# Pacing of the side work of an attention slot: complete at 0.8 of the slot in place of 0.74

## The chip, the cores and the metric

One core of one Trainium2 chip. The metric is device time in microseconds (us), the median of repeated executions. The engines are TensorE (PE in the profile: matmuls and transposes; PEld are its weight loads), VectorE (DVE), ScalarE (ACT), GpSimd (POOL) and SyncE (SP), which only issues transfers here.

## The reference

Input x is 8 images of 512 channels, 32x32 positions, f32. Two layers run one after the other, each on a group-normalised copy of its input and added to it:

```
x = x + cv2(concat(y0, y1, y2, y3))         # layer 0, input group_norm(x)
    y0, y1 = halves of silu(bn(conv1x1(gn(x))))          # "cv1", 512 -> 512
    z      = silu(bn(conv3x3(y)))                        # "cv1" of block i, 256 -> 256
    z      = attention(z): q, k, v = conv1x1(z); 4 heads of 64, 1024 positions
             softmax(q . (k + r) / 8) times v
    y_next = y + silu(bn(conv1x1(z)))                    # "m_cv2"; blocks i = 0, 1
    cv2    = silu(bn(conv1x1(...)))                      # 1024 -> 512
x = x + conv1x1(group_norm(x)), with masked, scaled and permuted weights   # layer 1
```

## The kernel before

**Slots, units, steps.** The two blocks of eight images are 16 *slots* (L737 to L741). The images go in pairs, in the order (first image, block 0), (second, 0), (first, 1), (second, 1). The attention of a slot is cut into four *units* (pair of heads, half of the query positions), and each unit into eight key tiles t, which are taken two at a time. The loop over slots runs over the four units j of a slot (from L1048 on). A unit does `top` (L524: the running maxima are transposed into a PSUM bank, L530, and reduced, L531), `spread` (L533: the negated maxima are transposed back into `mb`, L539), and then for each pair of key tiles `soften` (L544, DVE adds `mb` to the logits), `exponent` (L548, ACT; L555, POOL sums), `values` (L562, `po`, of the pair before) and the *next* unit's `logits` (L510, with the ACT copy L517 out of PSUM and the DVE maximum L522). `finish` and `divide` (L571 to L585) close the unit before. So the logits of the next slot begin in the last unit of this one, at its first pair of key tiles: they need that slot's q and k.

**Side work.** All that is not attention is fed between these steps by generators, which yield after every few matmuls and give their estimated time in us. `slot_filler` (L912 to L947) lists them for slot s: background work of other images (`bg.take`: first 1x1 convolutions, `cv2`, layer 1), the 1x1 convolution behind the attention (`conv_m2`), the 3x3 convolution of the next slot (`conv3`, L294: six products of 12 matmuls each, L313, over *planes* that DVE and POOL make from the input, L280 to L285 and L340 to L346), the next slot's q, k and v (`project`, L377, L405), and at the end as much background work as fills the slot up to `SHARE`, 103. The sum without that last entry is `needed`, the sum with it `total`. From the entries' estimates, `needed` is 8 + 7 + 9 + 32 + 7 + 21 = 84 in the slots whose next slot is a block 1 (s = 1, 2, 5, 6, 9, 10, 13, 14), 75 in the others, 68 in slot 0 and 15 in slot 15, which has no next slot.

**The pace.** `advance(share)` (L1041) pulls from that list until the done estimate reaches a goal, the larger of two: `share` of `total`, and a faster share of `needed`. A slot has 4 x 10 steps; with base = 10 j, `advance` is called at (base + 0.7)/40 ahead of `top`, (base + 1.4)/40 ahead of `spread`, (base + 2)/40 behind it, and (base + 4 + t)/40 behind each pair of key tiles. In the last unit (base 30) these are 30.7, 31.4, 32 (0.8 of the slot, right ahead of the pair in which the next slot's first logits are issued), 34, 36, 38 and 40 of 40.

**What sets the order on the engines.** The order in the program is the order on each engine. `pe_turn` (L196), `act_turn` (L188) and `in_turn` (L182) keep the attention's instructions, and the transforms of DVE, in the order in which they are written. A clock of estimated us (L743) starts further work when it is due: DVE's plane transforms by a list with a gap between its entries (`Spread`, L204), group norm's steps, and loads. `Background.take` (L867) overshoots by a part of a group and takes what it overshot from its next share (`over`, L870).

**PSUM.** Logits, transposed maxima, denominators and all side work share five banks (L63, `bank`, L68), which are used in turn; a group of matmuls can start only when ACT or DVE has emptied the bank five before it. `mb` and `po` have their own.

**ACT's functions.** `copy` and `mul` can run at any time; SiLU (L130) and the exponential (L548) use two tables, and a program that goes from one to the other contains a table load (ACT_TABLE_LOAD).

Of the kernel before, what the change touches and what calls it, by code (L numbers as in the profile page):

```python
# [39 lines left out]
def conv_preact_kernel(ctx: ExitStack, tc: tile.TileContext, x, cv1, cv2, mcv1, qkv, mcv2, bn, rw, rh, conv, s_in, t_in, out):  # L40
# [871 lines left out]
    def slot_filler(s):  # L912

        prev = slots[s - 1] if s else (None, 0)
        nxt = slots[s + 1] if s + 1 < len(slots) else (None, 0)
        todo, needed = [], 0.0

        def add(us, g):
            nonlocal needed
            todo.append((us, g))  # L920
            needed += us

        im, i = nxt
        add(8.0, bg.take(8.0))
        if im and i == 1:
            add(7.0, im.conv_m2(0))
            add(0.0, call(im.transform, 1, 2.0, 3.3))
            add(9.0, bg.take(9.0))
        products = im.conv3(i) if im else iter(())
        if prev[1] == 1:  # L930
            if im:
                add(21.3, (us for _, us in zip(range(16), products)))
            add(7.0, prev[0].conv_m2(1))
            add(0.0, call(lambda: finishing(prev[0])))
        if im:
            add(10.7 if prev[1] == 1 else 32.0, products)
            add(7.0, bg.take(7.0))
        if im:
            add(21.0, im.project(i))
        if s + 2 < len(slots) and slots[s + 2][1] == 0:  # L940
            add(0.0, call(slots[s + 2][0].load_y))
            add(0.0, call(slots[s + 2][0].transform, 0, 8.0, 3.3))
        rest = SHARE - needed if im else 70.0
        if rest > 0:
            todo.append((rest, bg.take(rest, wait=True)))
        total = sum(c for c, _ in todo)
        return needed, total, todo  # L947
# [77 lines left out]
    for s in range(len(slots)):  # L1025
        needed, total, todo = slot_filler(s)
        state = {"done": 0.0}

        def filler():
            for us, g in todo:  # L1030
                start = state["done"]
                for cost in g:
                    clock.tick(cost)
                    state["done"] += cost
                    yield

                state["done"] = max(state["done"], start + us)

        fill = filler()

        def advance(share):  # L1041
            goal = max(share * total, min(1.0, share / 0.74) * needed + 0.1)
            while state["done"] < goal:
                if next(fill, "end") == "end":
                    break

        steps = 4 * (KT + 2)
        for j in range(4):  # L1048
            u = units[4 * s + j]
            nxt = units[4 * s + j + 1] if 4 * s + j + 1 < len(units) else None  # L1050
            base = j * (KT + 2)

            advance((base + 0.7) / steps)
            u.top()
            clock.tick(0.9)
            advance((base + 1.4) / steps)
            u.spread()
            clock.tick(0.9)
            advance((base + 2) / steps)
            for t in range(0, KT, 2):  # L1060
                if before and t == 0:
                    before.finish()
                    clock.tick(0.9)
                u.soften(t)
                u.soften(t + 1)
                if t:
                    u.exponent(t)

                lag = u if t else before
                if lag:  # L1070
                    lag.values((t - 2) % KT)
                    lag.values((t - 1) % KT)
                    clock.tick(2.0)
                if before and t == 0:
                    before.divide(0)
                    before.divide(1)
                if nxt:
                    nxt.logits(t)
                    nxt.logits(t + 1)
                    clock.tick(2.0)  # L1080

                if not t:
                    u.exponent(t)
                u.exponent(t + 1)
                advance((base + 4 + t) / steps)
            before = u
        for _ in fill:
            pass
# [62 lines left out]
```

## Time and profile before

| what | value |
|---|---|
| median of 3 runs | 3153.09 us (3151.32 to 3154.78) |
| the profiled execution's own time | 3162.82 us |
| its span, first to last instruction | 3161.1 us |
| mean granted TensorE clock | 0.996 |
| PE busy | 3077.0 us (97%) |
| DVE busy | 2049.9 us (65%) |
| ACT busy | 1721.0 us (54%) |
| POOL busy | 1398.4 us (44%) |
| ACT table loads | 224, of 1283 ns each |

A row such as "L548 ACT ... x512 | 539.1, 1068 | 304.1" is a group of instructions of one line: how many, busy us together, mean ns of one, and the idle us of that engine ahead of them with what ended it. In a timeline row the first two numbers are the start and the duration of a run of like instructions, and brackets hold idle time ahead of it with the instruction that ended it.

### The profile page before, as it was taken

The numbers are of one execution on the slowest core, as the hardware profiler recorded it, in microseconds if no ns is written. First come the engines' busy times: TensorE is split into PE (matmuls) and PEld (weight loads), VectorE is DVE, ScalarE is ACT, GpSimd is POOL, SyncE is SP. The second block draws the span as 40 slices with busy tenths as digits, with TensorE's granted clock in tenths as the row PEclk, the third lists the DMA queues.
The fourth block names the chain that finished last, engine by engine and source line by source line (L and its number), as shares of the span: only waits on it lengthen the run. The fifth ranks groups of instructions, "written<-read, shape, count | busy, mean of one in ns | idle before, by whom it ended". The sixth has DMA issues, their size and how long they took to land.

```text
span 3161.1 us, 34185 instructions
## 1 busy us (share of the span) xinstructions
PE 3077.0 (97%) x11668; PEld 1515.3 (48%) x11668; DVE 2049.9 (65%) x2718; ACT 1721.0 (54%) x2349; POOL 1398.4 (44%) x1867
## 2 busy tenths in 40 slices
PE   7999999998999999999999999999999999999999
PEld 3645354454445454455445454454445454453333
DVE  5446577567667576667666676767666676767642
ACT  3245765855655555644656455544656455546621
POOL 2104444546444554455444454445444464444520
PEclk9999999999999999999999999999999999999999
DMA  8852352421233232424233332424233332413356
GB/s 289 292 182 74 130 180 87 153 77 63 88 116 131 79 128 71 149 84 148 84 116 130 114 127 70 153 85 136 91 110 130 120 120 70 150 64 120 120 205 217
DMA packets 142014, 399.35 MB, mean 126 GB/s; under 512 B 13072, under 2 KB 14352, under 8 KB 141840
## 3 DMA queue, kind: packets, MB, share of 16 engines
q1 hardware_dynamic: 141120, 396.94, 36.6%
q8 instruction: 92, 1.51, 0.2%
q14 instruction: 82, 0.67, 0.1%
q10 hardware_dynamic: 720, 0.23, 0.0%
HBM read 317.42 MB, written 79.69 MB: 126 GB/s over the span
## 4 chain that ended last, share of the span: by engine, by line
PE 75%; DVE 4%; ACT 4%; issue 2%; DMA 1%; POOL 1%; SPq 0%; ACTq 0%; DVEq 0%; POOLq 0%
PE cv L175 15%; PE m L313 13%; PE po L562 12%; PE lg L510 12%; PE l L175 7%; PE qk L175 6%; PE v L405 3%; PE m L175 3%; PE den L576 2%; PE mb L539 2%; PE mt L530 1%; ACT st L517 1%; DVE st L544 1%; ACT st L548 1%; DVE mx L522 1%
## 5 line engine op out<-in xcount | busy, mean ns | idle before, releaser
L555 POOL TENSOR_TENSOR sum<-sum,st 128x256 f32<-128x256 f32 x1536 | 1132.0, 771 | 552.1 <-ACT st L548 547.7
L522 DVE TENSOR_TENSOR mx<-mx,lg 128x512 f32<-128x512 f32 x768 | 477.8, 682 | 417.6 <-ACT st L517 417.4
L517 ACT COPY st<-lg 128x512 f32<-128x512 f32 x1024 | 525.0, 597 | 356.1 <-PE lg L510 331.7
L548 ACT ACTIVATE st<-st 128x1024 f32<-128x1024 f32 x512 | 539.1, 1068 | 304.1 <-DVE st L544 302.9
L544 DVE TENSOR_TENSOR st<-st,mb 128x1024 f32<-128x1024 f32 x512 | 604.4, 1215 | 60.2 <-PE mb L539 60.2
L555 POOL TENSOR_TENSOR sum<-st,st 128x256 f32<-128x256 f32 x256 | 185.1, 754 | 788.8 <-ACT st L548 788.8
L313 PE MATMUL m<-plane,w_m 128*128 128x256 f32 x2304 | 528.8, 383 | 4.9 <-ACT cv2s L130 2.7
L562 PE MATMUL po<-st,v 128*64 128x512 f32 x2048 | 497.8, 605 | 18.2 <-ACT st L548 16.2
L510 PE MATMUL lg<-q,k 64*128 64x512 f32 x2048 | 510.9, 617 | 2.9 <-ACT y L130 2.9
L313 PEld LDWEIGHTS m<-plane,w_m 128*128 128x128 f32 x2304 | 426.4, 189 | 129.5 <-issue 45.1
L175 PE MATMUL cv<-y,w_cv 128*128 128x512 f32 x1024 | 464.5, 599 | 7.9 <-ACT cv2s L130 4.6
L510 PEld LDWEIGHTS lg<-q,k 64*128 64x128 f32 x2048 | 177.3, 186 | 328.2 <-issue 267.4
L175 PEld LDWEIGHTS cv<-y,w_cv 128*128 128x128 f32 x1024 | 185.8, 190 | 248.1 <-issue 226.4
L562 PEld LDWEIGHTS po<-st,v 128*64 128x64 f32 x2048 | 128.8, 136 | 323.6 <-issue 237.3
L175 PE MATMUL cv<-x,w_cv 128*128 128x512 f32 x512 | 237.0, 610 | 10.6 <-ACT y L130 3.7
L175 PE MATMUL l<-x,w_l 128*128 128x512 f32 x512 | 236.9, 606 | 7.9 <-DVE mx L522 6.9
L175 PE MATMUL qk<-z,w_qkv 128*128 128x512 f32 x512 | 234.0, 600 | 1.4 <-DVE mx L522 1.4
L583 DVE RECIPROCAL rb<-rb 128x256 f32<-128x256 f32 x128 | 215.5, 1723 | 26.0 <-ACT rb L579 25.8
L531 DVE TENSOR_REDUCE nm<-mt 128x4 f32<-128x512 f32 x128 | 82.3, 684 | 144.7 <-PE mt L530 144.7
L579 ACT COPY rb<-den 128x512 f32<-128x512 f32 x64 | 37.3, 583 | 230.4 <-PE den L576 230.4
L175 PEld LDWEIGHTS cv<-x,w_cv 128*128 128x128 f32 x512 | 95.3, 194 | 132.0 <-issue 109.3
L175 PEld LDWEIGHTS l<-x,w_l 128*128 128x128 f32 x512 | 93.4, 191 | 130.4 <-issue 112.2
(145 smaller groups left out, 2408.8 us busy)
## 6 DMA issues: line engine op xcount, KB each, us to landing
w_m<-w_m SPq DMA_DIRECT2D x96, 768.0 KB, 4.8
w_cv<-in_cv SPq DMA_DIRECT2D x90, 512.0 KB, 3.5
y<-y SPq DMA_DIRECT2D x64, 512.0 KB, 4.8
x<-in_x SPq DMA_DIRECT2D x56, 512.0 KB, 5.2
y<-y SPq DMA_DIRECT2D x64, 256.0 KB, 3.5
k<-r SPq DMA_DIRECT2D x32, 512.0 KB, 3.6
res<-y SPq DMA_DIRECT2D x32, 512.0 KB, 4.0
xr<-in_x SPq DMA_DIRECT2D x32, 512.0 KB, 4.1
```

The costliest lines, as they stand in the source:

```text
L175: nc.tensor.matmul(ps, w, moving, start=(n == 0), stop=(n == len(terms) - 1))
L313: nc.tensor.matmul(ps[:, ts(co, 256)].rearrange("p (t x) -> p t x", x=F), w[:, co, c, dx], u[:, 9 * c : 9 * c + 8, dx : dx + F], start=(j ...
L405: nc.tensor.matmul(ps[:, ts(j, P)], z[:, c, ts(4 * j4 + j, P)], w[:, c, 512 + P * hp : 512 + P * hp + P], start=(c == 0), stop=(c == IT - 1),)
L510: nc.tensor.matmul(lg[h], self.k[r, ts(t, P)], self.q[r, self.hp, ts(self.half, HALF)], start=True, stop=True)
L517: act_turn(nc.scalar.copy(st[:, h], lg[h]))
L522: in_turn(nc.vector.tensor_tensor(self.mx[:, h], so_far[:, h], lg[h], ALU.max))
L531: nc.vector.tensor_reduce(self.nm[:, h], mt, AX.X, ALU.max, negate=True)
L544: in_turn(nc.vector.tensor_tensor(st, st, flat(self.mb), ALU.add))
L548: act_turn(nc.scalar.activation(st, st, AF.Exp))
L555: nc.gpsimd.tensor_tensor(flat(self.acc)[:, part], flat(so_far)[:, part], st[:, part], ALU.add)
L562: nc.tensor.matmul(self.po[HD * h : HD * h + HD], self.v[:, t, ts(h, HD)], self.st[t][:, h], start=(t == 0), stop=(t == KT - 1),)
L583: nc.vector.reciprocal(self.rb[:, r], self.rb[:, r])
```

## The change

The number by which the pace of `needed` is divided goes from 0.74 to 0.8. Nothing else is edited.

```diff
         def advance(share):
-            goal = max(share * total, min(1.0, share / 0.74) * needed + 0.1)
+            goal = max(share * total, min(1.0, share / 0.8) * needed + 0.1)
             while state["done"] < goal:
                 if next(fill, "end") == "end":
                     break
```

The instructions of the attention stay in their order, to the last of the 1216 steps in which they are written. The side work stays in its order too, and moves against them. The program has the same matmuls, DVE, POOL and transfer instructions as before. ACT's instructions stand in another order, and 236 table loads instead of 224 lie among them.

## The prediction

> **What bounds the kernel now.** I read the page's engine shares and its chain of waits first, then what PE waits for, then the stretches slot by slot, then the timeline around each stall. First the page:
>
> ```profile
> PE 3077.0 (97%) x11668; PEld 1515.3 (48%) x11668; DVE 2049.9 (65%) x2718; ACT 1721.0 (54%) x2349; POOL 1398.4 (44%) x1867
> ...
> PE 75%; DVE 4%; ACT 4%; issue 2%; DMA 1%; POOL 1%; SPq 0%; ACTq 0%; DVEq 0%; POOLq 0%
> ```
>
> PE is busy for 3077.0 of 3161.1 us. The edit takes no matmul away, so only the 84 us in which PE stands can move. PE's own waits (cause, us in total, times, longest):
>
> ```profile
> PE po L562 <- ACT st L548: 16.2, 14, 3.7
> ...
> PE l L175 <- DVE mx L522: 6.9, 3, 2.5
> ...
> PE cv L175 <- ACT cv2s L130: 4.6, 6, 0.8
> ```
>
> Each is a matter of filling: matmuls wait until ACT or DVE has worked off what PE issued just before, because too little side work stood between. That is what pacing moves. Which slots does it reach? The goal is the larger of `total` (103 per slot) and `needed` divided by the constant. Where `needed` is 84, the second was 84/0.74 = 113.5 per slot and becomes 84/0.8 = 105, still above 103: eight slots (1, 2, 5, 6, 9, 10, 13, 14). Where it is 75, the second was 75/0.74 = 101.4, already below 103: nothing changes there, but for the overshoot that the slot before hands on (slots 4, 8, 12). The stretches of slots 1, 2, 5, 6 (us, then PE busy; then the other engines):
>
> ```profile
> 398.30:579.20 180.90, 176.42 (x698) 88.13 (x697) 124.17 (x172) 121.16 (x162) 86.07 (x115) 1.00 0.38 128
> 579.20:747.00 167.80, 157.62 (x648) 79.42 (x646) 114.42 (x143) 106.03 (x145) 81.53 (x112) 0.99 0.29 99
> 1099.90:1280.80 180.90, 178.55 (x698) 88.34 (x697) 124.17 (x155) 98.44 (x135) 89.12 (x117) 1.00 0.32 106
> 1280.80:1458.80 178.00, 173.43 (x692) 86.76 (x691) 127.97 (x168) 95.61 (x135) 89.72 (x114) 1.00 0.37 125
> ```
>
> PE stands for 4.5, 10.2, 2.35 and 4.6 us in them; slots 9, 10, 13 and 14 give 2.3, 4.3, 2.3 and 4.1 in the same view. Together 34.6 us. Of slot 2's 10.2, four stalls of 2.3, 2.4, 1.3 and 1.6 us at 728 to 747 fall where the background has no work ready in either order, 7.5 us. So **at most 27 us, 0.9%, can be won**, and the clock (1.00 in six of the eight, 0.99 in slots 2 and 14) adds little.
>
> **The change, part by part.** In the affected slots the same side work stands later against the attention: by 1.7 to 2.6 us of matmuls in the slot's second unit, 3.9 to 5.2 in the third, up to 7.0 in the fourth, and level again as the next slot begins. Matmul time stays; what counts is which stall goes and which comes.
>
> (1) *A step that gains: first values behind new logits.* Before, in slot 6's last unit (PE and ACT):
>
> ```profile
> 1427.52 1.99 PE L510 MATMUL lg<-q,k 64*128 64x512 f32 x8
> ...
> 1428.73 2.05 ACT L517 COPY st<-lg 128x512 f32<-128x512 f32 x4 [2.20 <-PE lg L510]
> ...
> 1429.44 1.12 PE L175 MATMUL l<-x,w_l 128*128 128x512 f32 x2
> ...
> 1431.79 1.59 PE L562 MATMUL po<-st,v 128*64 128x512 f32 x6 [1.23 <-DVE mx L522]
> ```
>
> From the logits' end (1429.44) to `po` (1431.79) pass 2.35 us: ACT finishes four copies, then one exponential of 1.07. One matmul's two passes stand between, and PE idles 1.23. After the change two matmuls stand there. Slot 5 has that arrangement already, and shows what is left:
>
> ```profile
> 1248.26 2.02 PE L562 MATMUL po<-st,v 128*64 128x512 f32 x8 [0.37 <-ACT st L548]
> ```
>
> So 0.86 us are won in each of slots 6, 10, 14. In slots 4, 8, 12 the same wait carries a table load (1.28), is 0.48 long behind 3.29 us of side work, and gets about 1.3 us more: 0.48 won, three times, −1.4. There SiLU moves behind two exponentials and brings two table loads to each, which lie where ACT has room.
>
> (2) *A step that loses: the first product of the 3x3 convolution*, slots 5, 9, 13. Before, DVE makes its plane (L282) at 1137.70 to 1138.42, ahead of the maxima of the logits just issued, and PE waits 0.91 us for a bank:
>
> ```profile
> 1136.99 1.99 PE L510 MATMUL lg<-q,k 64*128 64x512 f32 x8
> 1139.89 2.43 PE L313 MATMUL m<-plane,w_m 128*128 128x256 f32 x10 [0.91 <-ACT cv2s L130]
> ```
>
> In the new order four maxima (1.27 us for two by the trace, 2.5 in all) stand on DVE ahead of L282. They begin with the logits at about 1138, so the plane is done at 1138 + 2.5 + 0.7 = 1141.2. PE starts at 1141.2 in place of 1139.89, with nothing else to run: +1.3. A wait of 0.16 at the sixth product goes. Net +1.1 each, **+3.3**. If DVE's plane comes early after all, this is 0.
>
> (3) *Slots 6, 10, 14, the rest.* The group behind the attention is split: one of its matmuls now waits for DVE's maxima for about 1.5 us where the next group waited 0.60, +0.9; layer 1's first group waits for a SiLU at about 2.6 where it waited 2.48 for DVE, +0.2; a wait of 0.27 ahead of a product goes. With −0.86 from (1): about 0 each, ±1.5, since each is a difference of two waits on two engines.
>
> (4) *Slots 1 and 2.* One `po` gets cover (−0.9, the same price as in slot 6), another stands behind 0.4 us of group norm where 2.35 are needed (+1.4 over what it waits now); four more changes between whole-array and half-array matmuls at about 0.1 us (start to start, against 0.43 a pass) are +0.4; the regrouped `conv_m2` gives between −0.8 and +0.8. Slot 1: +1, between −2 and +3. Slot 2 loses two waits of 0.3 and 0.5 and gains one of about 1: +0.3.
>
> (5) *ACT's table loads:* 236 against 224, 12 × 1.283 = 15.4 us of ACT, which is busy 54% of the span. They cost nothing where ACT's idle time ahead of copies and exponentials (331.7 and 302.9 us in the waits) takes them; otherwise each delays a `po` or a bank by 1.28. I count them with the steps above; all of them on the path would be +15.4. The trace shows no more than the load itself: a copy ends at 1647.87, the load runs at 1647.89 for 1.28, the exponential starts at 1649.19.
>
> The Trainium skill ("ScalarE: Activation LUTs", What ACT_TABLE_LOAD costs) gives about 1283 ns and a drain of some 1380 on top, and its decision table wants work grouped by table set; that speaks against this change. By its price the 12 loads would be 32 us of ACT, an estimate from that page; the trace has the 1283 and not the drain.
>
> (6) *Loads and transforms.* What is called at the end of `needed` (load of y and transforms for the slot after next, in slots 2, 6, 10, 14) comes some 9 us later, at 0.8 in place of 0.75 of a slot of 178 us. It is used after 0.2 × 178 + 8 = 44 us, against 8 + 8 × 3.3 = 34 by its own due times and 3.5 to 4.8 us for a landing: nothing. Uncovered it would be one DVE transform, 1.2 us each. Weight loads are issued on SP by the side work that uses them, and move with it; PE waits 0.4 us in all for w_m now. I take 0, within ±2.
>
> Sum: −1.4 + 3.3 + 0 + 1 + 0.3 + 0 = **+3.2 us**. Against the profiled execution's own 3162.82 that is 3166.0. It lies 9.7 above the median of the runs, 3153.09; carried over: **3156 us**, 0.1% more. A measurement of this kernel can tell about 0.2% (6.3 us) from no change, so this is "no change".
>
> **The rivals.**
> - *Faster: the thin last unit was the cost.* Before, nothing is due at 30.7, 31.4 and 32, so transposes, `mb`, denominators and first logits follow closely; afterwards up to 7 us of side work lies among them. If every new wait in (2) to (4) falls through and the stalls of slots 6, 10, 14 at layer 1 (2.48) and `cv2` (0.60) go as well, the sum is −1.4 − 3 × (0.86 + 2.48 + 0.6 + 0.27) − 0.5 − 3 = −17.5: about 3136. For it: these stalls are fillable. Against it: slots 5, 9, 13 show only 0.37 us of standing in this last unit, so there is little to cure there, and the waits of 2.48 and 0.60 lie in the slot's first unit, where the lag is small.
> - *Slower: ACT passes its table loads on.* Place: the exponential and the SiLU that frees a bank. Price 1.283 each; if all 12 reach PE, +15.4 on top of (2): about 3172. It decides as soon as the idle time ahead of ACT's next copy is below 1.28 us. For it: ACT is busy 121 of 181 us in slot 1, and five banks put the next matmul group right behind a SiLU. Against it: in slots 4, 8, 12, which take 6 of the 12, about 0.8 us of new cover is left over.
> - *It does little of what it says:* half of the slots go by 103 anyway, and −27 to +15 meet in the middle. This is my forecast's case, within ±6 us.
>
> **Chances.** Forecast's case (3147 to 3159) 0.47, mechanisms of both signs cancelling; slower, between it and the full price of the loads, 0.32; faster, down to the full filling, 0.21. So faster by over 0.2% 0.21, within 0.47, slower 0.32. The range leaves out the far ends of both rivals: 3141 (two thirds of the faster one, from the median) to 3170 (most of the slower one's 15.4). The forecast's case alone: 3147 to 3159.
>
> **What would show it.** (1): in slots 6, 10, 14 the first `po` of the next slot's unit idles about 0.4, not 1.2; in slots 4, 8, 12 the 0.48 is gone. (2): the first L313 of slot 5 waits for DVE (L282 or a maximum) and starts about 2.2 us after the logits' end. (5): 236 table loads, and PE's wait of `po` for ACT stays at or below 16.2 us; well above it the slower rival is right. Slots 5 and 6 together should last 358.9 + 1 us; 350 would mean the faster rival. Slots 3, 7, 11 must keep their 178 us; if they move, the pace of 103 does not govern them as I hold.

## The result, and the profile after

The changed kernel takes 3175.79 us (median of 6, 3173.36 to 3183.63) against 3153.85 for the kernel before: ratio 1.0073, interval 1.0058 to 1.0088, so 22 us slower. The prediction was 3156, with 3141 to 3170. The profiled execution took 3180.13 us, its span is 3178.4, 17.3 more than before's. From the page and from PE's waits (cause, us in total, times, longest):

```profile
PE 3085.5 (97%) x11668; PEld 1521.9 (48%) x11668; DVE 2046.8 (64%) x2718; ACT 1738.8 (55%) x2361; POOL 1389.6 (44%) x1867
```

```profile
PE l L175 <- ACT cv2s L130: 10.4, 3, 3.6
PE po L562 <- ACT st L548: 10.1, 8, 3.7
PE cv L175 <- ACT y L130: 7.1, 3, 3.3
PE m L313 <- DVE plane L282: 6.3, 4, 2.2
...
PE po L562 <- DVE mx L522: 4.6, 7, 2.3
```

Two things are to be seen. What the change was to help, values waiting for exponentials, did fall, from 16.2 us to 10.1. The fall is smaller than it looks: some of these waits are put down to the maxima in one profile and to the exponential in the other, and the two rows of `po` together go from 18.2 to 14.7. And PE is busy 8.5 us longer with the same 11668 matmuls: half of the 17.3 us are matmuls that ran slower, and the other half is standing.

Slot by slot (from the first transpose of a slot to that of the next, in us):

| slots | before | after | difference |
|---|---|---|---|
| 1 | 180.9 | 189.0 | +8.1 |
| 2 | 167.8 | 170.5 | +2.7 |
| 5, 9, 13 | 180.9 each | 181.1 each | +0.7 together |
| 6, 10, 14 | 178.0, 177.7, 179.3 | 180.2, 180.1, 182.1 | +7.3 |
| 4, 8, 12 | 173.4, 172.0, 172.0 | 172.8, 171.4, 171.4 | -1.9 |
| 3, 7, 11 | 179.5, 177.8, 177.8 | 179.0, 177.8, 177.8 | -0.5 |
| 0 and 15 | 185.9, 283.9 | 184.6, 286.3 | +1.1 |

The work of slots 0 and 15 keeps its order. Slot 15 lasted between 278 and 286 us in the profiles of all kernels here; I read nothing from these two. Single slots move between executions too: slots 4, 8 and 12 last 0.7 us more than before in the kernel below that has 0.8 in slots 5, 9 and 13 alone. Two places, slot 1 and the family 6, 10, 14, hold nearly all of it. The stretch of slot 6 in the changed kernel, with columns as in the prediction:

```profile
1289.20:1469.40 180.20, 175.30 (x692) 88.17 (x691) 127.16 (x168) 96.23 (x135) 87.37 (x114) 0.99 0.37 124
```

PE busy went from 173.43 to 175.30 us in it, PE standing from 4.6 to 4.9: here the loss is almost wholly slower matmuls. In slots 6, 10 and 14 together PE busy grew by 5.0 us and standing by 2.4. The place is the end of the slot's first unit (ACT, DVE and PE, from the logits on):

```profile
1324.17 2.34 DVE L544 TENSOR_TENSOR st<-st,mb 128x1024 f32<-128x1024 f32 x2
...
1324.79 1.99 PE L510 MATMUL lg<-q,k 64*128 64x512 f32 x8
...
1325.41 1.06 ACT L548 ACTIVATE st<-st 128x1024 f32<-128x1024 f32 x1 [2.84 <-DVE st L544]
...
1326.38 1.50 ACT L165 ACTIVATE x<-x,go_b,gr_b 128x512 f32<-128x512 f32 x2
...
1327.90 1.28 ACT L130 ACT_TABLE_LOAD   x1
1329.19 0.78 ACT L130 ACTIVATE cv2s<-cv,bn_b,bn_s 128x512 f32<-128x512 f32 x1
```

And PE alone behind it:

```profile
1330.03 5.40 PE L175 MATMUL l<-x,w_l 128*128 128x512 f32 x8 [3.24 <-ACT cv2s L130]
```

The logits end at 1326.8. The next group is layer 1's, and the bank whose turn it is was the last `cv2` group's. Its SiLU stands on ACT behind an exponential (which waits for DVE), two normalisations and a table load, and frees it at 1330. PE has stood 3.24 us, and then eight passes (each matmul of this f32 kernel is two rows of the trace, here called passes) take 5.40 us; eight such passes of `cv` take 3.70 in before's row at 1309.83 below. The granted clock from 1330.03 to 1333.48, over the slow passes, is 0.52; over the 3.2 us of standing it was 1.00. In slots 10 and 14 the row of layer 1 reads 5.11 behind 3.46, and 6.49 behind 3.65.

Why was it not so before? There layer 1's first two matmuls stood *ahead* of the last two pairs of logits (the same place in the kernel before, PE and the SiLU on ACT):

```profile
1307.91 1.99 PE L510 MATMUL lg<-q,k 64*128 64x512 f32 x8
1309.83 3.70 PE L175 MATMUL cv<-y,w_cv 128*128 128x512 f32 x8
1316.01 1.98 PE L175 MATMUL l<-x,w_l 128*128 128x512 f32 x4 [2.48 <-DVE mx L522]
1317.93 1.94 PE L562 MATMUL po<-st,v 128*64 128x512 f32 x8
...
1318.95 0.78 ACT L130 ACTIVATE cv2s<-cv,bn_b,bn_s 128x512 f32<-128x512 f32 x1
...
1319.80 1.99 PE L510 MATMUL lg<-q,k 64*128 64x512 f32 x8
1321.71 1.98 PE L175 MATMUL l<-x,w_l 128*128 128x512 f32 x4
```

Which bank each group has I worked out from the program and from what the rows wait for. The banks do not come strictly five groups later: layer 1's group is the fifth after the `cv2` group here (four logits were opened while that group ran), and yet it starts at 1316.01, while that group's SiLU ends only at 1319.73. The rows fit banks that come up again in the order in which the program empties them. Before, layer 1's group opened in a bank of the logits before (which is why it waited for DVE's maxima), and the last logits (key tile 7, second head) got the `cv2` bank, with four passes of layer 1, the values and three other logits as cover. In the changed kernel the four logits come directly between the two groups and use up the four other banks; layer 1 gets the `cv2` bank itself, and nothing is left to cover its SiLU.

### The profile page after: what moved, and what is told of

The parts are those of the page before. It is cut to its first block, busy times and chain, and to the rows that moved or that the text cites. A ratio compares the mean times of both kernels' runs of the same rounds, so it can differ in the third digit from the quotient of the medians.

```text
span 3178.4 us, 34191 instructions
## 1 busy us (share of the span) xinstructions
PE 3085.5 (97%) x11668; PEld 1521.9 (48%) x11668; DVE 2046.8 (64%) x2718; ACT 1738.8 (55%) x2361; POOL 1389.6 (44%) x1867
## 4 chain that ended last, share of the span: by engine, by line
PE 75%; DVE 5%; ACT 4%; issue 2%; DMA 1%; POOL 0%; SPq 0%; ACTq 0%; DVEq 0%
PE cv L175 15%; PE m L313 13%; PE po L562 12%; PE lg L510 12%; PE l L175 7%; PE qk L175 6%; PE v L405 3%; PE m L175 2%; PE mb L539 2%; PE den L576 2%; PE mt L530 2%; DVE st L544 1%; ACT st L517 1%; ACT st L548 1%; DVE mx L522 1%
## 5 line engine op out<-in xcount | busy, mean ns | idle before, releaser
L555 POOL TENSOR_TENSOR sum<-st,st 128x256 f32<-128x256 f32 x256 | 180.5, 737 | 819.8 <-ACT st L548 819.8
L562 PE MATMUL po<-st,v 128*64 128x512 f32 x2048 | 498.7, 605 | 15.2 <-ACT st L548 10.1
L175 PEld LDWEIGHTS cv<-y,w_cv 128*128 128x128 f32 x1024 | 186.2, 190 | 253.6 <-issue 237.8
```

Of the source, the lines that this page charges most:

```text
L175: nc.tensor.matmul(ps, w, moving, start=(n == 0), stop=(n == len(terms) - 1))
L555: nc.gpsimd.tensor_tensor(flat(self.acc)[:, part], flat(so_far)[:, part], st[:, part], ALU.add)
L562: nc.tensor.matmul(self.po[HD * h : HD * h + HD], self.v[:, t, ts(h, HD)], self.st[t][:, h], start=(t == 0), stop=(t == KT - 1),)
```

## The experiments

**Theory A**: the time goes by where groups of side work end against the logits. A group that opens right behind logits may get the bank that a SiLU at the end of ACT's queue has to free; a stall of about 3 us or more is paid again, when matmuls run at half rate behind it. **Rival B**: the 12 more table loads. **Rival C**: later side work is longer, evenly. Ratios are against the kernel before on the same chip.

**The change by slots.** Three kernels with 0.8 in some slots only:

```diff
-            goal = max(share * total, min(1.0, share / 0.8) * needed + 0.1)
+            goal = max(share * total, min(1.0, share / (0.8 if s in (6, 10, 14) else 0.74)) * needed + 0.1)
```

This is the first; the others have (1, 2) and (5, 9, 13) in the brackets.

> The kernel before with 0.8 in slots 6, 10 and 14 alone. 224 table loads, as before. Theory A (a group of layer 1 that starts right behind a pair of logits waits for the bank that the last cv2 group's SiLU empties, over 3 us, and TensorE then runs at half rate for some us): these three slots become 2.2, 2.35 and 2.8 us longer, as in the changed kernel, about +7 us in all against before, most of it with TensorE busy at half rate. Rival B (the change costs by its 12 more table loads on ScalarE): no loads are added, so within 2 us of before.

Measured 1.0040 (1.0024 to 1.0055). The three slots last 180.8, 181.6 and 178.3 us, against 177.0, 178.8 and 177.5 in the kernel below that leaves them alone: +7.3, as theory A has it, with not one table load more than before. Against before's own profile it is 5.7. The loss is in slots 6 and 10, where PE stands 3.86 and 3.69 us and slow passes follow; in slot 14 it stood 2.63, the eight passes took 3.70, and the slot is only 0.8 longer. The ratio is worth 12.6 us, 7.6 at its lower end; the rest is not in these slots, and I cannot place it.

> The kernel before with 0.8 in slots 1 and 2 alone. 230 table loads, 6 of the 12. Theory A: a stall over 3 us behind the last logits of slot 1's first unit, with half-rate matmuls behind it, and one at the first product of slot 2: +8 and +2.5 us, together about +10.5. Rival B: half of the loads, so half of the change's time, +11 at most, spread over the waits of values for exponentials rather than in one place. The two are told apart by the place, not by the sum.

Measured 1.0041 (1.0026 to 1.0055). Slots 1 and 2 last 359.1 us together, against 350.3 and 351.1 in the two kernels that leave them alone: +8 to 9. The two stalls are where theory A has them: 2.94 us behind the last logits of slot 1's first unit, with eight passes in 5.29 behind it, and 2.19 at the first product of slot 2. That they make up the loss is not shown by this run.

> The kernel before with 0.8 in slots 5, 9 and 13 alone. 224 table loads. The prediction on record had +1.1 us for each of these (3.3 in all); the changed kernel's profile shows 0.2 each. Theory A and rival B both expect within 1.5 us of before; above 3 us the plane's wait at the first product would be the dear step after all.

Measured 1.0002 (0.9994 to 1.0011): nothing. The three parts add up to 0.83%, against 0.73% for the whole.

**One pair of matmuls back across the logits.** The changed kernel and

```diff
+            if s in (6, 10, 14) and share == 8 / steps:
+                goal += 1.7
```

> The changed kernel, with the goal raised by 1.7 us at one step of slots 6, 10 and 14 (share 8/40): one pair of layer 1's matmuls stands ahead of the last two pairs of logits of that unit instead of behind them, and nothing else moves on TensorE. All 236 table loads stay. Theory A: the group no longer begins behind the logits, its bank is an earlier one; the waits of 3.4 to 3.8 us fall to 2.6 or less, the half-rate matmuls behind them go, and 2 to 2.5 us come back in each of the three slots: 6 to 7.5 us faster than the changed kernel, some +15 against before. Rival B: no change, +22 against before.

Measured 1.0044 (1.0032 to 1.0056). PE at the same place in slot 6:

```profile
1324.12 1.88 PE L175 MATMUL l<-x,w_l 128*128 128x512 f32 x4
1325.93 1.94 PE L562 MATMUL po<-st,v 128*64 128x512 f32 x8
1327.80 1.99 PE L510 MATMUL lg<-q,k 64*128 64x512 f32 x8
1329.72 1.98 PE L175 MATMUL l<-x,w_l 128*128 128x512 f32 x4
```

No idle time in brackets and four passes in 1.98: stall and slow matmuls are both gone. The slots last 177.8, 178.5 and 179.0 us, 7.0 less than in the changed kernel. All 236 loads are still there. For slots 6, 10 and 14 theory A is shown, and B and C fall. (Slot 1 was left as it is; it stood 3.34 us, its eight passes behind took 3.70, the full rate, and it lasted 188.5.)

**Is half of the price the clock?** The changed kernel with 2.6 us of matmuls that add zero, in the gap:

```diff
...
                     nxt.logits(t + 1)
+                    if s in (6, 10, 14) and j == 0 and t == 6:
+                        u.keep_busy(3)
...
```

`keep_busy(3)` is 3 x 2 matmuls, ones times a zero column, into the open `po`; its definition and the column of zeros are left out here.

> The changed kernel with three more pairs of matmuls (ones times a zero column, added into the open group of values, so that the sums stay as they are) right behind the last logits of the first unit in slots 6, 10 and 14, 2.6 us in all, inside the wait of 3.4 to 3.8 us. The wait of layer 1's group for ScalarE stays; TensorE no longer stands so long. If half of the price is the clock (theory A), the half-rate matmuls behind it go: 1.4 to 2.6 us back in each of the slots, 5 to 6 us in all, +16 against before. If the clock plays no part, the same +22, or up to 1 us more where the added work sticks out.

Measured 1.0031 (1.0019 to 1.0042). Slot 6 again:

```profile
1325.79 2.81 PE L577 MATMUL po<-zeros,ones 128*64 128x512 f32 x12
1329.73 3.70 PE L177 MATMUL l<-x,w_l 128*128 128x512 f32 x8 [1.13 <-ACT cv2s L132]
```

Layer 1's group still waits for the same SiLU, until 1329.7. But PE stands 1.13 us and not 3.24, and its eight passes take 3.70 and not 5.40; in slots 10 and 14 it stands 0.60 and 0.24, with 3.70 again. The slots last 179.1, 178.6 and 178.6: 6.0 us less than in the changed kernel, for work that computes nothing. The slower matmuls came with the standing, and they were most of the price. (The ratio fell by more than these slots show, 0.42%; the runs were on another chip, and the intervals allow 0.16% to 0.69%.)

**Slot 1.** The shift by a pair in slots 1, 6, 10, 14.

> As the kernel with a pair of matmuls pulled ahead at share 8/40 in slots 6, 10 and 14, and the same in slot 1 as well, where the changed kernel waits 3.3 us for a SiLU behind the last logits of the first unit and then runs at half rate. 234 table loads. Theory A: slot 1 falls from 189 to about 184.5 us, so 4 to 5 us less than the kernel with three slots mended (+13 against before there): about +9, ratio near 1.003. Rival B (table loads): two loads fewer, 3 us at most, and not in that place.

Measured 1.0022 (1.0012 to 1.0033), 0.2% less than with three slots on another chip, more than was expected; but slot 1 lasts 187.3 us in the profile, only 1.2 less than there, 1.7 less than in the changed kernel, and still 6.4 more than before. The stall of 3.3 us is gone, 1.23 is left ahead of the convolution's first product, and the first `conv_m2` group waits 1.84, which waited 1.16 in the changed kernel. So this stall explains little of slot 1's length, and theory A's 4 to 5 us did not come in that place. What was in front of the awaited SiLU in the changed kernel (ACT):

```profile
433.22 1.28 ACT L130 ACT_TABLE_LOAD   x1
434.51 0.78 ACT L130 ACTIVATE y<-cv,bn_b,bn_s 128x512 f32<-128x512 f32 x1
435.31 1.28 ACT L548 ACT_TABLE_LOAD   x1
436.60 1.06 ACT L548 ACTIVATE st<-st 128x1024 f32<-128x1024 f32 x1
437.68 1.28 ACT L130 ACT_TABLE_LOAD   x1
438.97 0.78 ACT L130 ACTIVATE y<-cv,bn_b,bn_s 128x512 f32<-128x512 f32 x1
```

Two SiLUs that need one load stand here apart, with an exponential between: two loads, 2.6 us, directly ahead of the SiLU that PE waits for. So in this one place loads lie on the path, as rival B has it. With the pair shifted both SiLUs run behind one load; the run moves the matmuls and the loads together and does not tell the two apart.

**The constant itself.**

> The constant 0.77, halfway. 232 table loads. Theory A: time goes by which groups of side work end right ahead of logits; in this order no group of layer 1 begins behind logits with a cv2 group ahead of it, so slots 6, 10 and 14 stay within 1 us of before, and the sum is -3 to +8, not halfway by rule. Rival B: 8 of 12 loads, +15. Rival C (the later the side work, the longer, evenly): +11, half of it.

Measured 1.0014 (1.0003 to 1.0025), +4.4 us. Slots 6, 10 and 14: 178.7, 178.1, 178.8. Inside theory A's bounds; below half, and below B's.

> The constant 0.9: 84/0.9 = 93 is below 103, so the pace of total holds everywhere. 242 table loads. Theory A: layer 1's group begins right behind logits with a cv2 group ahead of it in slots 6, 10 and 14, as with 0.8, so these keep the longer time: +10 to +25, by place. Rival B: 18 more loads than before, +33. Rival C: further along the same line than 0.8, about +24 (the pace is bound at 103 from 0.816 on).

Measured 1.0047 (1.0030 to 1.0065), +15 us: less than at 0.8, with 18 more loads than before. B and C are off. But it is no clean win for A either: slots 6, 10, 14 keep the wait of layer 1's group (11.6 us in all) and yet last 178.5, 180.6 and 178.3. What differs is the rate behind the wait (slots 6, 10 and 14):

```profile
1335.13 3.70 PE L175 MATMUL l<-x,w_l 128*128 128x512 f32 x8 [3.95 <-ACT cv2s L130]
...
2042.57 5.40 PE L175 MATMUL l<-x,w_l 128*128 128x512 f32 x8 [4.32 <-ACT cv2s L130]
...
2751.28 3.70 PE L175 MATMUL l<-x,w_l 128*128 128x512 f32 x8 [3.34 <-ACT cv2s L130]
```

Behind 3.95 and 3.34 us the passes ran at full rate (granted clock 1.00), and only slot 10, with slow passes, kept the longer time. So the half rate decides the price here as well, but it does not follow every such stall. Slots 5, 9, 13 are *shorter* than before, by 1.1 each. The loss lies in slots 1 and 2 (191.6 and 174.8). From 0.74 over 0.77 and 0.8 to 0.9 the ratios run 0, +0.14%, +0.73% (+0.64% when run again, below), +0.47%: not an even slope.

**Only the last unit.** 0.74 up to share 0.6, then a line to 0.8:

```diff
-            goal = max(share * total, min(1.0, share / 0.8) * needed + 0.1)
+            part = share / 0.74 if share <= 0.6 else 0.6 / 0.74 + (share - 0.6) / 0.2 * (1 - 0.6 / 0.74)
+            goal = max(share * total, min(1.0, part) * needed + 0.1)
```

> What the change does in the last part of the slots alone: 0.74 up to share 0.6, then a straight line to be complete at 0.8. 224 table loads. Theory A: the group ends in the first two units stay as before, so the long stalls of slots 1, 2, 6, 10 and 14 do not come; the fuller last unit wins about 0.9 in each of slots 6, 10, 14 and 0.5 to 0.6 in each of 4, 8, 12: -1 to -6 us against before. Rival C (later side work costs): half or more of +22.

Measured 0.9994 (0.9983 to 1.0006), -1.9 us: no difference that can be told, and half of +22, as rival C has it, is excluded. Slots 6, 10 and 14 have 176.2, 176.4 and 176.6 us, 1.3 to 2.7 less than before; slots 4, 8 and 12 gained nothing (174.1, 172.7, 172.7), against what I expected of them, and slot 1 took 187.3.

The changed kernel once more, beside it:

> The changed kernel once more, on the chip of the two above, as a measure for them: ratio 1.006 to 1.009 against before, and slots 6, 10 and 14 above 180 us.

Measured 1.0064 (1.0046 to 1.0082); 182.0, 180.5 and 180.7 us.

**Can theory A be used?** Eleven pairs moved by it in the kernel before (a table of +1.7 or -1.7 by slot and share):

> The kernel before (0.74), with eleven single pairs of matmuls moved across four logits or values, where the profile of before shows a stall behind a pair of logits: one pair of a cv2 group later at share 6/40 of slots 6, 10, 14 (stalls of 2.4 to 2.6 us), one pair of the next group earlier at 6/40 of slot 2 (2.2 us and half rate behind it), at 36/40 of slot 0 (2.2), of slots 5, 9, 13 (0.9 each) and at 34/40 of slots 6, 10, 14 (1.4, of which 0.9). 220 table loads. Theory A (place of group ends against logits): those stalls are 18 us together; with what comes up behind them, 8 to 18 us faster than before. Rival B (table loads): 4 fewer, 5 us at most. Rival C (mean position of the side work): nothing, since every pair moves by less than 10 us and both ways.

Measured 0.9998 (0.9989 to 1.0007): the gain expected did not come. The stalls aimed at went: slots 5 and 9 are 0.7 us shorter, slots 6 and 10 by 1.7, and the ones in slots 0 and 2 are gone as well. In the whole profile PE stands 73.8 us in place of 84.1, but is busy 4.9 us longer. Slot 13 gained nothing, and slot 14 is 1.4 longer than before. The wait went on to the next in turn. In slot 6 the SiLU's bank falls to the logits:

```profile
1318.71 1.98 PE L510 MATMUL lg<-q,k 64*128 64x512 f32 x6
1321.76 1.12 PE L510 MATMUL lg<-q,k 64*128 64x512 f32 x2 [1.07 <-ACT cv2s L130]
```

In slot 14 the same wait is 1.39, half rate follows, and four passes of layer 1 behind the logits take 3.78 where four took 1.98 in slot 6 before.

And slot 1, whose order is as before, lasted 186.2 us, against 180.9 to 183.3 in four kernels that leave it alone (before's among them): reached 3 us earlier, it stands 2.87 us at its first `conv_m2` group, which waited 0.91 before, with half rate behind it; ACT's normalisations there wait for DVE. That it was reached earlier is not shown to be the cause: reached at 396.8 to 396.9 us, this group waited 1.16 in the changed kernel and 3.00 in the next one.

> A kernel put together by slot from what the profiles of the others show: 0.74 in slots 1 and 2, 0.9 in slots 5, 9 and 13 (179.8 us there in place of 180.9), in slots 6, 10 and 14 the straight line to 0.8 behind share 0.6 and one pair of a cv2 group later at share 6/40 (1.7 us each by either alone, so up to 3.4 together). 230 table loads, 6 more than before. Theory A (place of group ends against logits): 1.1 + 1.7 to 3.4 us three times and 0.6 in each of slots 4, 8, 12: 8 to 15 us faster than before, ratio 0.9955 to 0.9975. Rival B (table loads): +11. Rival C (later is longer): slower than before.

Measured 0.9988 (0.9976 to 1.0000), -4 us by the ratio and -2 by the medians: the lowest ratio here, at the edge of what can be told, and short of the 8 to 15 expected. Slots 5, 9 and 13 kept their gain (179.7, 179.7, 179.9), but in slots 6, 10 and 14 the two gains did not add: 179.4, 178.5, 178.7, again with logits waiting for the SiLU, up to 1.7 us. Slots 4, 8 and 12 stayed as before.

## Why the prediction was wrong

The step that failed is **(3)**, and with it two sentences that all steps rest on: that "only the 84 us in which PE stands can move", and "Matmul time stays". PE was busy 8.5 us longer with the same matmuls, half of the 17.3. I put layer 1's wait for a SiLU at "about 2.6 where it waited 2.48, +0.2". I had the right wait, on the right instruction, but too short: it measured 3.24, 3.46 and 3.65 us, with an exponential that waited for DVE, two normalisations (1.50) and a table load ahead of the SiLU. Above all I priced a stall at its length and put the slow matmuls behind it at nothing. There eight passes took 1.4 to 2.8 us more, 5.9 in the three slots. For slots 6, 10 and 14 the step said 0 and the profile shows +7.3; one pair of matmuls moved back takes 7.0 away, and zero-work in the gap 6.0. The other waits of the step went the forecast way: the split group behind the attention waits 1.20 (forecast 1.5), and the 0.27 is gone.

**(4)** failed as well: slot 1 was put at +1, between -2 and +3, and measured +8.1. Its worst stall, 3.27 us behind the unit's last logits and half rate after it (eight passes in 5.13), was not in my list. But with one pair moved there the stall went and slot 1 still lasted 187.3 us. Standing in slot 1 rose from 4.5 to 9.1 us and PE busy from 176.4 to 179.9. What makes up slots 1 and 2, more than half of the whole loss, was not separated and stays open; the profile shows waits of 1.2 us in the split `conv_m2`, of 2.2 for the plane in slot 2 and of 1.8 at q and k.

**(1)** was right: the first values behind new logits idle 0.39 us in slot 6 (forecast 0.4, from 1.23), and slots 4, 8, 12 won 0.6 each (forecast 0.48), which is no more than they move between executions; the wait of 0.48 itself is gone. With **(2)** the wait was right and the sum was not: the first product in slots 5, 9, 13 waits for plane L282, 1.38 us where it waited 0.91, with two matmuls of `cv2` ahead of it where I had "nothing else to run". In slot 5 a wait of 0.92 for the maxima's reduction came and one of 0.77 for a SiLU went, neither on my list, and the slots lost 0.2 and not 1.1. The alternative stated there, 0, was the nearer, by luck.

**(5)** held outside slot 1: its own test, `po` waiting no more than 16.2 us for ACT with 236 loads, came out at 10.1 (14.7 against 18.2 with the waits put down to the maxima). Slots 4, 8 and 12 took six loads and did not become longer. On **(6)** nothing speaks against: PE waits 2.1 us for y in place of 1.5, and 0.7 for weights in place of 0.4.

The rivals missed it too. The slower one had the sign, at 3172, but by loads as such. My upper end, 3170, was most of its 15.4 us, with no slow matmul in it. The profile before did hold the warning: behind the 2.13 us stall at 609.73 seven passes of `cv` take 4.97 us.

## What to carry to other kernels

When work is paced against other work, ask not how early or late it stands on average, but which group opens right behind the instructions that use up the banks, and whose slow release it thereby inherits; two matmuls on the other side of four logits decided 2 us per slot here. Beside its length, give a stall that may grow to some 3 us the price of slow matmuls behind it: 1.4 to 2.8 us in the changed kernel, and nothing in some executions. And a mended stall is won only when the next in turn has slack: removing some 17 us of stalls by this rule gave nothing that could be measured.

## What the runs showed of the hardware

Matmuls at half rate follow most long stalls of PE, not all. In slots 0 to 14 of all profiles here there are 20 stalls of 3.0 to 5.1 us; behind 16 of them the granted clock fell to half, behind 3.05, 3.34, 3.34 and 3.95 it did not. Of 84 stalls between 2 and 3 us, 35 were followed by half rate, and some shorter ones too, such as the 1.39 above. In these slots the trace's record of the clock has 58 stretches at 0.5: 50 last 3.41 us and 8 last 6.83. The clearest pair is one wait for a SiLU in slot 0, in the profile before and then in the one after:

```profile
380.33 5.42 PE L175 MATMUL cv<-x,w_cv 128*128 128x512 f32 x12 [2.16 <-ACT y L130]
```

```profile
376.95 7.11 PE L175 MATMUL cv<-x,w_cv 128*128 128x512 f32 x12 [2.16 <-ACT y L130]
```

The same twelve passes behind the same 2.16 us took 1.69 us longer the second time. The order of that slot is the same in both kernels, so this is chance of the execution. It is likely part of why executions of one kernel differ: those of the kernel before lie between 3149 and 3168 us on one chip, and the longer ones tend to have the lower mean clock (0.995 at 3168, 0.998 at the shortest).

The Trainium skill ("TensorE: Matmul & The Clock Gate", Part 1) has the clock halved after about 3.4 us of idle time, seen in a window that runs freely, and about as long to come back. The stretches of 3.41 us, or twice that, agree with the time to come back, and a free window would let chance in. The idle time does not agree: half rate followed 2.16 and 1.39 us of standing here, and did not follow 3.95.

Matmuls that add zero, 2.8 us of them put into the gap, kept the rate in all three slots where they were tried: eight passes in 3.70 us each time.
